# A pipeline of six steps instead of four for the expert tiles of a mixture-of-experts block

## The chip, the core and the metric

The kernel runs on one core of one Trainium2 chip. The metric is the time of one execution on the device in microseconds (us); the median of the runs is what counts. The engines are called by short names. PE is the matrix engine, and PEld its weight load, which overlaps it. DVE is the vector engine, ACT the scalar engine, POOL the GpSimd engine. SP issues DMAs only; SPq and ACTq are the DMA-issuing sides of SP and ACT.

## The reference

The reference is a cross-attention layer and a mixture-of-experts feed-forward layer, each added to its input. The change touches only the second, which is, cut to what matters:

```
def _L0_ffn_ref(x, Wg, W1, W2, W3, Ws1, Ws2, Ws3):
    # T = 4096 tokens, D = 256, H = 128, E = 32 experts, TOP_K = 4
    xf = x.reshape(T, D)
    weights, indices = jax.lax.top_k(softmax(xf @ Wg), TOP_K)
    y = jnp.zeros_like(xf)
    for e in range(E):
        pos = jnp.nonzero(pair_expert == e, size=C, fill_value=P)[0]
        tok, w = ...                      # the tokens that chose e, their weights
        xg = xf[tok]
        out = (silu(xg @ W1[e]) * (xg @ W3[e])) @ W2[e] * w[:, None]
        y = y.at[tok].add(out)
    z = (silu(xf @ Ws1) * (xf @ Ws3)) @ Ws2      # shared expert, 256 wide
    return (y + z).reshape(B, S, D)
```

All numbers are 32-bit floats.

## The kernel before, in words

The 4096 tokens are eight blocks (blk 0 to 7) of 512. Attention runs over all blocks first and lasts to about 390 us of the profile. While it runs, POOL scatters each token's normalised row into a DRAM tensor `xr`, four times, once behind each expert that the token chose. The rows of one expert then lie together and are cut into tiles of 128 rows. There are 128 tiles that are always computed (NM_ = 128), and up to 32 more, in groups of eight, whose number is known only at run time. The inputs at hand need two such groups, 144 tiles in all.

The change lies in the stage that computes those tiles. Each tile passes four functions, named in the list `steps`:

- `expert_in`: PE transposes the 128 by 256 tile of rows `g` into a PSUM bank `pgT` (two instructions); DVE copies it to `gT`.
- `expert_mid`: PE multiplies `gT` by the expert's W1 and W3, side by side, into the bank `peh` (four instructions in the trace); ACT takes Silu of the first half into `h`, DVE multiplies `h` by the second half.
- `expert_turn`: PE transposes `h` into the bank `phT`; ACT copies it to `ehT`.
- `expert_out`: PE multiplies `ehT` by W2 into the bank `py` (two instructions); ACT scales the result by the pair's weight into `y`; POOL scatters `y` with an indirect DMA into the DRAM tensor `ys`, at the place of token and choice.

The loop over `j` is a software pipeline. In iteration j, tile j is in step 0, tile j-1 in step 1, tile j-2 in step 2 and tile j-3 in step 3; a step's result waits in `made` for the next iteration. The program order is kept for every engine: all that is emitted inside `as_written()` runs on its engine in the order in which it was emitted. So each engine is a queue, and a late instruction holds all that stands behind it.

There are two such loops. The first runs over tiles 0 to 127. The second stands inside `tc.Switch`, a branch on the number of further groups, and runs over tiles 128 to 143 here. Between them the pipeline runs empty and is filled again. Other work is placed in the loops by iteration number:

- `fetch(j)` (every eight iterations) makes SP issue eight DMAs, one per tile, that bring the rows of a group of eight tiles into the buffer `g` (two buffers). It also loads the expert numbers into PE's registers.
- `find(j, step)` works out on DVE, in three iterations, the weights `own` and places `place` of a group.
- `shared_in`, `shared_mid`, `shared_out`, `shared_add` compute the shared expert for one block: products `ph` on PE, Silu on ACT, product with the second half on DVE, products `pz` on PE, addition to `y0` on DVE. Their input `sx` is brought back from DRAM by `fetch_shared(blk, engine)`, into one of three buffers of the pool `sxp`. Blocks 1 and 2 are computed in and around the two loops, 3, 4 and 5 in the tail.
- `take(i)` brings the four results of 128 tokens back from `ys` into a buffer `gx` (SP, 512 KB, three buffers). It must wait until the scatters of the tiles concerned have landed: tiles below NE_ = 80 for the first twelve, all tiles below 128 for the next eight. `add_taken` adds a `gx` to `y0` on DVE in three additions, the last of which also issues the next `take`.

After the branch comes the tail. SP gathers the results of the last tokens (`gather`, six DMAs of 1 MB into `gy`), PE computes the shared expert of blocks 3, 4 and 5, DVE adds up, and ACT issues the stores to `out`.

Of the kernel before, what the change touches and what calls it, by code (L numbers as in the profile page):

```python
# [9 lines left out]
F32 = mybir.dt.float32  # L10
# [6 lines left out]
P = 128  # L17
# [13 lines left out]
def kernel(  # L31
# [23 lines left out]
    nc = tc.nc  # L55
# [5 lines left out]
    KC = D // P  # L61
# [4 lines left out]
    H = W1.shape[2]  # L66
# [5 lines left out]
    NM_ = T * TOPK // P  # L72
# [4 lines left out]
    NE_ = NA + NE  # L77
# [3 lines left out]
    RG = 8  # L81
# [15 lines left out]
    def bank(name):  # L97
        return ps.tile([P, 512], F32, tag="bank", name=name)
# [476 lines left out]
    def fetch_shared(blk, engine):  # L575
        sxs[blk] = sxp.tile([P, KC, TB], F32, tag="sx", name=f"sx_{blk}")
        engine.dma_start(sxs[blk], xnd[blk])
# [3 lines left out]
    def shared_in(blk, f, act):  # L581

        if f == 0:
            hTs[blk] = hs.tile([P, HS // P, TB], F32, tag="hT", name=f"hT_{blk}")
        xnT = sxs[blk]
        ph = [bank(f"ph{i}_{blk}_{f}") for i in range(2)]
        for i in range(2):
            for k in range(KC):
                mm = nc.tensor.matmul(  # L589
                    ph[i],  # L590
                    ws13[:, k, i, f * P : (f + 1) * P],
                    xnT[:, k, :],
                    start=(k == 0),
                    stop=(k == KC - 1),
                )
                if i == k == 0:
                    began[0] = mm.ins.name
        sg = hs.tile([P, TB], F32, tag="sg", name=f"sg_{blk}_{f}", bufs=2)

        nc.scalar.activation(sg, ph[0], act, scale=0.5 if act == AF.Tanh else 1.0)  # L600
        sgs[blk, f] = sg, ph, act

    def shared_mid(blk, f):
        sg, ph, act = sgs.pop((blk, f))
        if act == AF.Silu:
            nc.vector.tensor_tensor(hTs[blk][:, f, :], ph[1], sg, ALU.mult)
        else:
            nc.vector.scalar_tensor_tensor(sg, sg, 1.0, ph[0], ALU.add, ALU.mult)
            nc.vector.scalar_tensor_tensor(hTs[blk][:, f, :], sg, 0.5, ph[1], ALU.mult, ALU.mult)
# [468 lines left out]
        sends(3)  # L1078
        shared_add(z)
    late_stack.close()  # L1080
    sxp = ctx.enter_context(tc.tile_pool(name="sxp", bufs=3, side="right"))

    def registers(table, j0, engine, most):
        _, vals = nc.values_load_multi_w_load_instructions(
# [10 lines left out]
    bp = bp_stack.enter_context(tc.tile_pool(name="bp", bufs=2, reuse_waits="tile"))  # L1095
# [60 lines left out]
    def expert_in(j, _):  # L1156
        g = groups[j // RG][0]
        pt = bank(f"pgT_{j}")
        for k in range(KC):
            nc.tensor.transpose(pt[:, k * P : (k + 1) * P], g[:, j % RG, k * P : (k + 1) * P], ident)  # L1160
        gT = bp.tile([P, KC, P], F32, tag="gT", name=f"gT_{j}")
        nc.vector.tensor_copy(gT.rearrange("p k t -> p (k t)"), pt[:, :D])  # L1162
        return gT

    def expert_mid(j, gT):
        ph = bank(f"peh_{j}")
        for k in range(KC):
            nc.tensor.matmul(  # L1168
                ph[:, : 2 * H],
                gT[:, k, :],  # L1170
                we[:, ds(ev[j] * EW + k * 2 * H, 2 * H)],
                start=(k == 0),
                stop=(k == KC - 1),
            )
        h = bp.tile([P, H], F32, tag="h", name=f"h_{j}")
        nc.scalar.activation(h, ph[:, :H], AF.Silu)  # L1176
        nc.vector.tensor_tensor(h, ph[:, H : 2 * H], h, ALU.mult)  # L1177
        return h

    def expert_turn(j, h):  # L1180
        pt = bank(f"phT_{j}")
# [60 lines left out]
    def store(hb, engine=nc.scalar):  # L1242
# [3 lines left out]
            out[r0 : r0 + HC * P, :].rearrange("(c p) d -> p c d", p=P), y0[blk][:, c0 : c0 + HC, :]  # L1246
        )

    steps = [expert_in, expert_mid, expert_turn, expert_out]
    made = {}  # L1250
    BL = BM - 1
    adds, adds_l = (
# [2 lines left out]
    with as_written():  # L1255
        fetch(0)
        fetch_shared(1, nc.sync)
        for j in range(NM_ + len(steps)):
            if j % RG == 1 and j + RG - 1 <= NM_:
                fetch(j + RG - 1)  # L1260
            if j in (4 * RG + 4, 5 * RG + 4, 6 * RG + 4):
                fetch_shared(j // RG - 2, nc.sync)
            if j == NE_ + 3:
                for i in range(3):
                    take(i)
            for i, step in enumerate(steps):
                jj = j - i
                if 0 <= jj < NM_:
                    made[jj, i + 1] = step(jj, made.pop((jj, i), None))
            if j in (2, 5, 8, 11):  # L1270
                next(tz)

            for blk, j0 in ((1, 3), (2, NM_)):
                if j == j0:
                    shared_in(blk, 0, AF.Silu)
                    sends(3)
                if j == j0 + 1:
                    shared_mid(blk, 0)
                    shared_in(blk, 1, AF.Silu)
                    sends(3)  # L1280
                if j == j0 + 2:
                    shared_mid(blk, 1)
            if j == 6:
                shared_out(1)
                sends(2)
            assert not left or j < 6
            if j == 7:
                shared_add(1)
            if NE_ + 8 <= j < NM_:
                for i, step in adds[:1]:  # L1290
                    add_taken(i, step, BE * NC)

                    if step == TOPK // 2 and i % HC == 0 and HC <= i <= 2 * NC:
                        store(i // HC - 1, nc.sync)
                del adds[:1]
            if j < NM_ and j % RG in (0, 1, 2):
                find(j // RG * RG, j % RG)
            if j == NM_ - 2 * RG:
                more = {
                    e: nc.values_load(  # L1300
                        tabs["more"],
                        engines=[e],
                        min_val=0,
                        max_val=(NJ - NM_) // RG,
                        skip_runtime_bounds_check_because="at most as many tiles as are laid out",
                    )
                    for e in mybir.ALL_ENGINES
                }
                tc.switch_hint(more, (NJ - NM_) // RG + 1, label="more")
            if j == NM_ + 2:  # L1310
                fetch_shared(5, nc.scalar)
    assert not adds
    ahead = groups[NM_ // RG][0]
    for n in tc.Switch(more, (NJ - NM_) // RG + 1, hint="more"):
        end = NM_ + n * RG
        groups.clear(), made.clear()
        adds = list(adds_l)
        groups[NM_ // RG] = [ahead]
        del ev[NM_ + RG :]
        with as_written():  # L1320
            for i in range(3):
                take(BE * NC + i)
            for j in range(NM_, end + len(steps)):
                if j % RG == 1 and j + RG - 1 < end:
                    fetch(j + RG - 1)
                for i, step in enumerate(steps):
                    jj = j - i
                    if NM_ <= jj < end:
                        made[jj, i + 1] = step(jj, made.pop((jj, i), None))
                if j < end and j % RG in (0, 1, 2):  # L1330
                    find(j // RG * RG, j % RG)
                if j == end:
                    shared_out(2)
                if j == end + 1:
                    shared_add(2)
                if j >= NM_ + 6:
                    for i, step in adds[: 1 + j % 2]:
                        add_taken(i, step, BL * NC)
                    del adds[: 1 + j % 2]
            for i, step in adds:  # L1340
                add_taken(i, step, BL * NC)
# [26 lines left out]
    with as_written():  # L1368
        come = {hb: gather(hb) for hb in (12, 13, 14, 15, 10, 11)}
        shared_in(3, 0, AF.Silu)  # L1370
        shared_in(3, 1, AF.Silu)
        shared_mid(3, 0)
        store(4)
        shared_mid(3, 1)
        shared_in(4, 0, AF.Silu)
        store(5)
        shared_out(3)
        gathered(*come[12])
        store(12)
        shared_mid(4, 0)  # L1380
        shared_in(4, 1, AF.Silu)
        shared_add(3, store)
        gathered(*come[13])
        store(13)
        shared_mid(4, 1)
        shared_in(5, 0, AF.Silu)
        shared_out(4)
        gathered(*come[14])
        store(14)
        shared_mid(5, 0)  # L1390
        shared_in(5, 1, AF.Silu)
        shared_add(4, store)
        gathered(*come[15])
        shared_mid(5, 1)
        store(15)
        gathered(*come[10])
        shared_out(5)
        gathered(*come[11])
        shared_add(5, store)
# [55 lines left out]
```

## Time and profile before

| what | value |
|---|---|
| median of 3 runs | 764.09 us (763.78 to 767.37) |
| profiled execution, its own time | 762.74 us |
| span of its profile | 761.0 us, so 1.74 us lie around it |
| mean granted clock of PE | 0.989 |
| PE busy | 720.0 us (95%) |
| DVE, ACT, POOL busy | 478.2, 402.3, 404.1 us |
| first and last product of `expert_mid` | 453.9 and 714.8 us |
| last instruction of the two loops on DVE | ends at 723.86 us |
| tail on PE | 724.0 to 754.2 us |

The rows of the profile give a start in us from the span's start, a duration, the engine, the line of the kernel, the operation with its output and input, and in square brackets the idle time of the engine before it with what ended it. "x4" behind a row means that four instructions were merged into it. Matmuls overlap in the pipeline of PE, so a row's duration is longer than the time until the next one starts; the times between starts are what counts.

### The profile page before, as it was taken

Reading aid. Unit: us, or ns where it says so; the run is one execution under the profiler, and the core shown is the slowest. Engines: PE = TensorE matmul, PEld = TensorE weight load, DVE = VectorE, ACT = ScalarE, POOL = GpSimd, SP = SyncE. Lnnn points to the kernel's source line nnn. Section 1 sums busy time; section 2 is a strip of 40 time slices with the busy share of each in tenths; the row PEclk is TensorE's granted clock in tenths of the full one; section 3 lists DMA queues with packets and bytes.
Section 4 is the critical chain, followed back from the end, with each engine's and each line's share of the span. In section 5 each row is a group of like instructions: output and inputs, shape, how many; then the busy total and the mean of one; then the engine's idle time right before and its main releaser. Section 6 shows DMA issues by size and latency. Waiting matters only on the chain. (4 is left out here: it accounts for less than half of the span.)

```text
span 761.0 us, 13078 instructions
## 1 busy us (share of the span) xinstructions
PE 720.0 (95%) x3515; PEld 536.6 (71%) x3515; DVE 478.2 (63%) x1368; ACT 402.3 (53%) x1730; POOL 404.1 (53%) x492
## 2 busy tenths in 40 slices
PE   7999999999999999999987779999999999999996
PEld 5866777677777767777763457788888887876754
DVE  2965565777877878776757433644545466645766
ACT  2658567666777576766553002455555555544310
POOL 1003343346777878777786655565565555553500
PEclk9999999999999999999998989999999999999999
DMA  8930000402217131513136451555746579847594
GB/s 284 342 113 1 1 1 1 132 7 87 100 59 253 47 127 52 170 59 120 74 97 210 140 189 65 159 173 183 224 161 195 166 262 311 258 127 244 186 342 163
DMA packets 78599, 111.98 MB, mean 147 GB/s; under 512 B 8949, under 2 KB 63667, under 8 KB 78515
## 3 DMA queue, kind: packets, MB, share of 16 engines
q1 hardware_dynamic: 60319, 68.76, 29.4%
q0 software_dynamic: 13056, 36.72, 13.0%
q10 hardware_dynamic: 5140, 5.55, 2.1%
q8 instruction: 32, 0.52, 0.3%
q14 instruction: 52, 0.43, 0.2%
HBM read 62.36 MB, written 48.64 MB: 146 GB/s over the span
## 5 line engine op out<-in xcount | busy, mean ns | idle before, releaser
L327 ACT ACTIVATE p<-sc,mx 128x77 f32<-128x77 f32 x512 | 159.5, 352 | 93.2 <-DVE mx L319 93.2
L1197 POOL DMA_INDIRECT ys<-y,place x144 | 138.9, 964 | 124.1 <-ACT y L1196 102.0
L1168 PE MATMUL peh<-we,gT 128*128 x576 | 150.7, 385 | 6.9 <-DVE gT L1162 5.4
L378 PE MATMUL po<-we,pT 128*128 128x256 f32 (+1 forms) x640 | 147.3, 383 | 4.8 <-DVE pT L365 3.4
L555 POOL DMA_INDIRECT xr<-xn,row x128 | 128.1, 1000 | 41.1 <-issue 33.1
L342 POOL TENSOR_TENSOR p<-p,su 128x385 f32<-128x385 f32 (+1 forms) x96 | 91.1, 974 | 97.5 <-DVE su L337 76.5
L311 PE MATMUL sc<-we,qT 128*128 128x385 f32 (+1 forms) x384 | 138.9, 509 | 0.9 <-POOL qT L297 0.9
L378 PEld LDWEIGHTS po<-we,pT 128*128 128x128 f32 (+1 forms) x640 | 118.4, 190 | 27.1 <-DVE pT L365 5.8
L327 ACT ACTIVATION_READ_ACCUMULATOR p<-sc,mx 128x1 f32 x512 | 119.3, 233 | 0.0
L1168 PEld LDWEIGHTS peh<-we,gT 128*128 128x128 f32 x576 | 99.2, 192 | 16.7 <-DVE gT L1162 6.5
L311 PEld LDWEIGHTS sc<-we,qT 128*128 128x128 f32 x384 | 71.1, 189 | 54.3 <-issue 27.7
L1176 ACT ACTIVATE h<-peh 128x128 f32<-128x128 f32 x144 | 40.0, 278 | 116.0 <-PE peh L1168 76.3
L1177 DVE TENSOR_TENSOR h<-peh,h 128x128 f32<-128x128 f32 x144 | 41.9, 291 | 87.1 <-ACT h L1176 80.2
L1192 PE MATMUL py<-we,ehT 128*128 x288 | 86.1, 381 | 0.0
L1196 ACT ACTIVATE y<-py,own 128x256 f32<-128x256 f32 x144 | 68.3, 475 | 17.8 <-PE py L1192 2.0
L319 DVE TENSOR_REDUCE mx<-sc 128x5 f32<-128x385 f32 (+1 forms) x96 | 54.3, 576 | 32.8 <-PE sc L311 30.1
L1162 DVE COPY gT<-pgT 128x256 f32<-128x256 f32 x144 | 60.5, 420 | 19.5 <-PE pgT L1160 9.1
L1160 PE MATMUL pgT<-ident,g 128*128 128x128 f32 x288 | 55.1, 274 | 1.3 <-DMA g<-xr 0.5
L1160 PEld LDWEIGHTS pgT<-ident,g 128*128 128x128 f32 x288 | 40.1, 142 | 17.2 <-issue 2.3
L1192 PEld LDWEIGHTS py<-we,ehT 128*128 128x128 f32 x288 | 43.6, 191 | 11.6 <-issue 0.8
L589 PE MATMUL ph<-sx,ws 128*128 128x512 f32 x96 | 46.0, 628 | 1.6 <-DVE y L1236 1.0
L360 PEld LDWEIGHTS pp<-ident,p 128*128 128x128 f32 x320 | 36.1, 139 | 11.4 <-issue 5.5
(227 smaller groups left out, 927.3 us busy)
## 6 DMA issues: line engine op xcount, KB each, us to landing
g<-xr SPq DMA_DIRECT2D x144, 136.0 KB
gx<-ys SPq DMA_DIRECT2D x20, 512.0 KB
gy<-ys SPq DMA_DIRECT2D x6, 1024.0 KB
xr<-y SPq DMA_DIRECT2D x1, 4352.0 KB
y<-in_x SPq DMA_DIRECT2D x8, 512.0 KB
xnd<-xnT SPq DMA_DIRECT2D x6, 512.0 KB
we<-in_W SPq DMA_DIRECT2D x8, 384.0 KB
out<-y ACTq DMA_DIRECT2D x12, 256.0 KB
```

Source lines behind the costliest of these rows:

```text
L311: nc.tensor.matmul(sc[:, : (h1 - h0) * SK], qTs[blk][:, k, o : o + P], mq[:, b, k, h0 * SK : h1 * SK], start=(k == 0), stop=(k == KC - 1),)
L319: nc.vector.tensor_reduce(mx[:, h0:h1], sv, AX.X, ALU.max, negate=True)
L327: nc.scalar.activation(probs[t][:, h, :], sv[:, h - h0, :], AF.Exp, bias=mx[:, h : h + 1], accum_out=su[:, h : h + 1],)
L342: nc.gpsimd.tensor_tensor(p[:, h0:h1, :], p[:, h0:h1, :], su[:, h0:h1].unsqueeze(2).to_broadcast([P, h1 - h0, SK]), ALU.mult,)
L378: nc.tensor.matmul(po[:, :D], pT[:n, i, :], vo[b][:n, i, :], start=(i == 0), stop=(i == KT - 1))
L555: sct = nc.gpsimd.indirect_dma_start(out=xr, out_offset=bass.IndirectOffsetOnAxis(ap=row[:, i : i + 1], axis=0), in_=xn[:, c, :], in_offse ...
L1160: nc.tensor.transpose(pt[:, k * P : (k + 1) * P], g[:, j % RG, k * P : (k + 1) * P], ident)
L1162: nc.vector.tensor_copy(gT.rearrange("p k t -> p (k t)"), pt[:, :D])
L1168: nc.tensor.matmul(ph[:, : 2 * H], gT[:, k, :], we[:, ds(ev[j] * EW + k * 2 * H, 2 * H)], start=(k == 0), stop=(k == KC - 1),)
L1192: nc.tensor.matmul(py[:, :D], hT, we[:, ds(ev[j] * EW + KC * 2 * H, D)], start=True, stop=True)
L1196: nc.scalar.activation(y, py[:, :D], AF.Identity, scale=own[:, i, 1:2])
L1197: sent = nc.gpsimd.indirect_dma_start(out=ys, out_offset=bass.IndirectOffsetOnAxis(ap=place_[:, i : i + 1], axis=0), in_=y, in_offset=None,)
```

## The change

`steps` gets two more entries. A new function, `expert_rest`, hands its input on and issues nothing; it stands once behind `expert_in` and once behind `expert_mid`. In iteration j, tile j is transposed, tile j-2 gets its first products, tile j-4 is turned and tile j-5 leaves. `gT` and `h` get three buffers each instead of two; the pool `sxp` has two buffers instead of three. The loops run two iterations longer at their ends, and what hung on iteration numbers is moved:

- `fetch_shared(4)` is no longer issued from SP in iteration 52, but from ACT in iteration 130, where `fetch_shared(5)` was; that one is issued from ACT in the tail, behind the two `shared_in` of block 3, whose buffer it takes.
- the first `take` moves from iteration 83 to 85, and the additions of taken results from 88..127 to 90..129.
- `shared_out(2)` and `shared_add(2)` move from the first and second iteration behind the last tile to the fifth and sixth.

```
-    sxp = ctx.enter_context(tc.tile_pool(name="sxp", bufs=3, side="right"))
+    sxp = ctx.enter_context(tc.tile_pool(name="sxp", bufs=2, side="right"))
...
-        gT = bp.tile([P, KC, P], F32, tag="gT", name=f"gT_{j}")
+        gT = bp.tile([P, KC, P], F32, tag="gT", name=f"gT_{j}", bufs=3)
...
-        h = bp.tile([P, H], F32, tag="h", name=f"h_{j}")
+        h = bp.tile([P, H], F32, tag="h", name=f"h_{j}", bufs=3)
...
+    def expert_rest(j, it):
+
+        return it
...
-    steps = [expert_in, expert_mid, expert_turn, expert_out]
+    steps = [expert_in, expert_rest, expert_mid, expert_rest, expert_turn, expert_out]
...
-            if j in (4 * RG + 4, 5 * RG + 4, 6 * RG + 4):
+            if j in (4 * RG + 4, 5 * RG + 4):
                 fetch_shared(j // RG - 2, nc.sync)
-            if j == NE_ + 3:
+            if j == NE_ + 5:
                 for i in range(3):
                     take(i)
...
-            if NE_ + 8 <= j < NM_:
+            if NE_ + 10 <= j < NM_ + 2:
                 for i, step in adds[:1]:
                     add_taken(i, step, BE * NC)
...
             if j == NM_ + 2:
-                fetch_shared(5, nc.scalar)
+                fetch_shared(4, nc.scalar)
...
-                if j == end:
+                if j == end + 4:
                     shared_out(2)
-                if j == end + 1:
+                if j == end + 5:
                     shared_add(2)
...
         shared_in(3, 0, AF.Silu)
         shared_in(3, 1, AF.Silu)
+        fetch_shared(5, nc.scalar)
         shared_mid(3, 0)
```

## Prediction

> **What bounds the kernel now.** I read the engines' busy time by stretches first. In the middle of the expert stage the first two numbers say all: PE is busy 136.00 of 136.00 us, at the full clock.
>
> ```profile
> 487.00:623.00 136.00, 136.00 (x754) 114.94 (x753) 69.19 (x234) 76.16 (x252) 78.88 (x82) 1.00 0.61 194
> ```
>
> The timeline of PE there repeats every 1.63 us: 0.22 (pgT) + 0.87 (peh) + 0.11 (phT) + 0.43 (py) between starts. The six-step order issues the same instructions in the same order, only of older tiles, so these 136 us don't move. What can move is where the period is longer, or PE waits. The timeline of PE, and of DVE and ACT where they hold it:
>
> ```profile
> 453.85 1.97 PE L1168 MATMUL peh<-we,gT 128*128 x4 [3.90 <-DVE gT L1162]
> 481.35 1.13 PE L1168 MATMUL peh<-we,gT 128*128 x4 [1.10 <-DVE eq L1122]
> 628.89 0.28 ACT L1176 ACTIVATE h<-peh 128x128 f32<-128x128 f32 x1 [2.44 <-PE peh L1168]
> 629.55 0.33 PE L1182 MATMUL phT<-ident,h 128*128 128x128 f32 x1 [1.04 <-DVE h L1177]
> 688.41 1.13 PE L1168 MATMUL peh<-we,gT 128*128 x4 [0.69 <-DVE gT L1162]
> 699.79 0.41 PE L1160 MATMUL pgT<-ident,g 128*128 128x128 f32 x2 [0.55 <-DMA g<-xr]
> ```
>
> In four of these PE waits for gT or h, which the change makes a step earlier; in the last one for rows from DRAM. Then the chain that ended last: it doesn't begin on PE, but on SP's queue, and it passes through the fetch of tiles 136 to 143. The line before the final PE row is DVE's last addition inside the branch; PE's second product of block 3 starts 0.14 us behind it.
>
> ```profile
> 699.04 3.56 DMA g<-xr
> 702.60 0.33 DVEq L1122
> ...
> 703.84 0.34 DVE gT L1162
> 704.19 0.04 issue
> 704.23 1.13 PE peh L1168 x4
> ...
> 723.43 0.43 DVE y L1236
> 723.86 0.14 issue
> 724.00 8.82 PE ph L589 x20
> ```
>
> Why that fetch is late: SP's queue holds the takes of iteration 128 before it, and these wait for the last scatter of tile 127 (POOL 688.07). SP resumes at 692.13, issues three gx, then g from 694.41; tile 136 is transposed at 699.79, 11.72 us after that scatter began.
>
> **Part by part, first loop.** The rests issue nothing. In the steady state gT is ready 1.0 us before its product (copy ends 501.15, product 502.16) and h 0.83 us before its transpose (500.57 to 501.40); both get 1.63 us more.
> Start: the third tile's two transposes move into the wait that ends at 453.85 (the late `shared_add` on DVE ahead of gT isn't touched). They cost 0.42 at 455.61. Bounds 0.2 to 0.4, I take 0.3.
> At 481.35 the period is 2.97 instead of 1.63; DVE's eight table operations had delayed gT by less than the new slack: 1.34 gone.
> At 628.89 ACT is 2 us late and the period is 3.41: 1.78. Here only part goes: the copy to ehT stands behind the same late Silu and has no step of rest, and its product would wait from 628.46 to about 629.35. 0.9 stays, 0.88 goes (nothing to 1.78, should the late Silu fall elsewhere).
> Seven periods of 1.70 to 1.73 (478.38, 483.08, 632.62, 644.62, 646.35, 655.20, 656.93) are DVE backlog: 0.64 in all.
> The periods of 2.15 at 639.66 and 2.24 at 653.48 follow PE's register loads in iterations 105 and 113, ahead of its transposes: they stay. Sum of the first loop: 0.3 + 1.34 + 0.88 + 0.64 = 3.16.
>
> What else moves there costs nothing, with these covers. The first takes stand two iterations later on SP's queue, ahead of the fetch for tile 96: its issue goes from 608.14 to about 608.5 (605.11 + 3.26 - 1.6 for the gx, 1.3 to issue them, 0.4 to 0.9 until the fetch). Tile 96 is due at 620.4, and 11.72 us would still be met. sx 4 leaves SP (0.46 us at 547.07) and takes the slot of sx 5 on ACT's queue. Its buffer is that of block 2, whose products end before it is issued; it is needed 40 us later. One buffer less in `sxp` makes block 3 wait for block 1, read by about 470 and refilled at 534. The additions have 40 iterations as before. POOL's scatters come two iterations later and POOL is idle 0.67 us in each.
>
> **The emptying before the branch.** `shared_in(2)` now stands ahead of the last turns, so nothing covers them: turn, out, turn, out, out are 2x0.11 + 3x0.43 = 1.51 us of PE. ACT must copy ehT, scale y (0.47), copy and scale again in that order; counted with the rows at 499.77 to 500.52, the last product ends 2.08 after the first turn: 0.57 lost. So tile 127 leaves PE at 687.12 - 3.16 + 0.57 = 684.5 instead of 687.12. POOL gets three results at once (0.96 + 0.30 each, as at 624.44 and 625.74). Its last scatter starts 1.94 us behind PE, at 686.5; before it was 0.95.
>
> **The branch.** Up to the transposes of tile 136 PE now has 8 transposed tiles, 6 first products, 4 turns, 3 outs: 1.74 + 5.20 + 0.43 + 1.30 = 8.67 us, and about 0.64 until the first gT is copied as at 688.41: it is through at 693.8. The rows come 11.72 us after the scatter, at 698.2. PE stands 4.4 us, where it stood 0.55. Behind that it has 8 transposed tiles, 10 first products, 12 turns, 13 outs and `shared_out(2)`: 1.74 + 8.67 + 1.28 + 5.63 + 3.45 = 20.77, with 0.57 for the uncovered turns 21.34. It ends at 719.5. The wait of 0.78 at 704.23 (DVE held by `find` until all rows had landed) is gone, for gT is two iterations ahead.
> The end: DVE has `shared_add(2)` and two additions left, 1.8 us after PE, where six additions ran from 719.87 to 723.86 before. Block 3's second product starts at 719.5 + 1.95 = 721.5 instead of 724.00: 2.5 us gained. The tail keeps its 37.0 us.
>
> **sx 5 in the tail.** ACT issues it when block 3 is read, 5.2 us into the tail; it is needed 10.3 us later, at 739.55 on the old clock. Alone, at 687.40, 0.45 of its 0.52 MB were through by 690: about 3.3 us. Beside the gathers, ACT's queue moved 0.26 MB from 731 to 735 in 1 KB packets while SP's moved 1.24 in 4 KB ones. At that worst share it takes 8 us plus the landing, about 10: just in time. With 4 KB packets I take 5 to 6 us: cost nothing. ACT's wait before the issue delays only a store and no Silu, since the next is due 1.8 us later.
>
> Sum: 761.0 - 2.5 = 758.5 of span, 760.2 with the 1.74 around it. This execution lay 1.35 below the median, so the forecast is 764.09 - 2.5 = **761.6**. Own range 759.5 to 763.8: the gain of the first loop can be 1.2 to 4.2, the landing 1 us either way.
>
> **The clock.** The 4.4 us that PE stands could cost more than themselves. Granted clock by half microseconds:
>
> ```profile
> 453.50:454.00 0.50, 0.15 (x1) 0.15 (x2) 0.50 (x3) 0.00 (x0) 0.00 (x0) 1.00 0.00 0
> 454.00:454.50 0.50, 0.50 (x2) 0.41 (x3) 0.23 (x1) 0.00 (x0) 0.00 (x0) 0.51 0.00 0
> ```
>
> After idle times of 4.57 (to 437.03) and 3.90 (to 453.85) the clock was 0.50 for 3.3 us, a loss of 1.65. The falls are at 436.95, 454.0 and 757.9, and their distances are 5 and 89 times 3.41: the clock is judged at fixed beats, and a beat has to be idle nearly whole (3.25 of 3.41 at 454.0). An idle time of 4.4 holds such a beat in about a third of the cases, so I leave the loss out of the sum.
> The Trainium skill ("TensorE: Matmul & The Clock Gate", its table of practical rules) speaks against the change more bluntly: no idle gaps of PE above some 3 us between bursts, since one idle window halves the clock. By that rule the sum would be 763.3; by the beats of the trace it is 761.6. The phase of the next run decides, and no row can give it.
>
> **The rivals.**
> The clock falls at tile 136: 761.6 + 1.65 = 763.3. For it: both long waits before tiles did so. Against: the beat. 0.20.
> The rows of tile 136 are not late: the takes are through sooner, or the scatter lands faster when nothing else moves. PE keeps its 4.4 us: 757.2. For it: the landing to SP at the branch's end took only 1.6 us (722.84 to 724.43), against 3.1 here. Against: three gx, 1.5 MB, stand before g either way. 0.12.
> Slower than before: sx 5 comes late. If it waits behind all gathers (6.28 MB, through at about 744.2 by the bytes per stretch) it lands at 745.7, 6.1 behind 739.55, and the clock falls too: 761.6 + 6.1 + 1.65 = 769.4. It decides from 10.3 us after issue. Against: the stores on ACT's queue moved while gathers did. 0.12.
> The stalls return elsewhere: late instructions with no cause in the profile (2.19 at 452.78 on DVE, 2 us at 628.89 on ACT) fall at other places, and the slack of ehT, which got no rest, is used up: gain eaten, 764 to 766. 0.10.
> The forecast holds with 0.46.
>
> **Chances.** A measurement tells about 0.5% here, 3.8 us: 760.3 and 767.9 are the marks. Faster: the rows in time, 0.12, and the lower quarter of the forecast, 0.12: 0.24. Slower: sx 5, 0.12, and a fifth of the returned stalls, 0.02: 0.14. Within: 0.62. The range from 757.0 to 767.5 leaves out half of the rows in time (0.06) and sx 5 (0.12).
>
> **What would show it.** Right: no wait at the fellows of 481.35; tile 136's transposes with an idle time of 3 to 5 us on a DMA; tile 127's scatter about 2 us behind its product; `shared_out(2)` last before the tail; DVE's last addition within 2 us of it; no wait in block 5's first product. Wrong: PE waits for ehT in many periods, a period other than 1.63 in the middle, or the tail longer than 37 us.

## The result, and the profile after

The changed kernel is slower by 0.39%: 766.53 us median of 20 runs (762.21 to 771.62) against 762.84 of 20 runs of the kernel before (760.51 to 767.37), ratio 1.0039, 95% interval 1.002 to 1.0057. The forecast was 761.6, which was 2.5 us below the median of three runs at hand then (764.09); the time lies 3.7 us above the kernel before. The profiled execution took 764.69 us, its span is 762.9, its mean granted clock 0.984 (762.74, 761.0 and 0.989 before).

The busy time by stretches first: the middle of the stage is what it was, PE busy without a gap at the full clock (the number in third place from the end).

```profile
487.00:623.00 136.00, 136.00 (x754) 114.89 (x753) 68.53 (x235) 75.80 (x251) 79.72 (x83) 1.00 0.59 190
```

Then PE's timeline, the rows with the waits.

```profile
446.52 1.22 PE L617 MATMUL pz<-ws,hT 128*128 128x256 f32 x2 [4.29 <-DVE hT L606]
...
456.27 1.13 PE L1168 MATMUL peh<-we,gT 128*128 x4 [2.35 <-issue]
...
630.00 0.70 PE L1196 MATMUL py<-we,ehT 128*128 x2 [0.81 <-ACT ehT L1188]
...
699.78 0.41 PE L1160 MATMUL pgT<-ident,g 128*128 128x128 f32 x2 [2.93 <-DMA g<-xr]
...
724.24 1.10 PE L589 MATMUL ph<-sx,ws 128*128 128x512 f32 x2 [1.21 <-DVE y L1240]
```

The wait at 481 is gone, the late Silu at 629 now costs 0.81 us (before ehT), and tile 136 waits for its rows, all as the prediction had it. But PE waits 4.29 us at 446.52, where the same products began without a wait before (at 445.21; the wait of 4.57 ahead of them, at 437.03, is 2.34 here). The first product stands at 456.27 and not at 453.85, although DVE, which it waits for, has nothing new to do ahead of it, and PE only the third tile's two transposes. The wait at 446.52 isn't DVE's alone: ACT, DVE and POOL all pause and begin again within 0.03 us of each other, with no releaser that the profile can name.

```profile
445.77 0.69 DVE L606 TENSOR_TENSOR hT<-ph,sg 128x512 f32<-128x512 f32 x1 [10.82 <-issue]
445.80 0.60 ACT L600 ACTIVATE sg<-ph 128x512 f32<-128x512 f32 x1 [6.01 <-remote]
445.79 0.96 POOL L555 DMA_INDIRECT xr<-xn,row  x1 [2.93 <-remote]
```

And in front of block 3 PE waits for DVE with both products. Two rows more show the end of the first loop, the last product of tile 127 on PE and the start of its scatter on POOL:

```profile
686.18 0.70 PE L1196 MATMUL py<-we,ehT 128*128 x2 [0.27 <-ACT ehT L1188]
688.61 0.96 POOL L1201 DMA_INDIRECT ys<-y,place  x1 [0.30 <-issue]
```

The granted clock by half microseconds shows what the wait at tile 136 cost beside itself. PE is idle from 696.85 to 699.78, and the clock is halved for the beat from 700.9 to 704.3:

```profile
700.50:701.00 0.50, 0.50 (x4) 0.40 (x3) 0.15 (x1) 0.00 (x0) 0.00 (x0) 0.90 1.09 398
...
703.50:704.00 0.50, 0.50 (x2) 0.30 (x2) 0.50 (x3) 0.00 (x0) 0.41 (x1) 0.50 0.12 49
704.00:704.50 0.50, 0.50 (x3) 0.41 (x2) 0.50 (x2) 0.17 (x1) 0.00 (x0) 0.69 0.13 49
704.50:705.00 0.50, 0.50 (x5) 0.40 (x5) 0.50 (x3) 0.39 (x3) 0.00 (x0) 1.00 0.65 230
```

The chain that ended last shows the same place: PE's work carries it to 694, then the fetch, then slow products (the four of peh take 1.71 us of the chain, where 0.87 is usual).

```profile
693.82 0.54 PE peh L1168 x3
694.36 5.29 DMA g<-xr
699.65 0.14 issue
699.78 0.41 PE pgT L1160 x2
...
702.59 1.71 PE peh L1168 x4
```

**Time lost at half clock.** Each run has its time and its mean granted clock. From them I work out, for a set of runs, the time lost, (1 - clock) x time, and the net time, time - lost. A beat of 3.41 us at half clock loses 1.7. (This counts lost time as if all of it lay on the path. Ahead of the expert tiles, where PE waits anyway, it costs less, and behind PE's last product nothing: there the profiles of before and after lose 1.6 and 2.0 us.) The runs went to chips of two kinds: on the slower ones the kernel before takes 762 to 765 us, on the faster ones 746 to 747 (medians). Both kernels, on one chip of each kind (means):

| chip | kernel | us | clock | lost | net |
|---|---|---|---|---|---|
| slower | before (27 runs) | 764.57 | 0.9870 | 9.94 | 754.63 |
| slower | after (12) | 768.87 | 0.9815 | 14.22 | 754.65 |
| faster | before (23) | 746.62 | 0.9948 | 3.86 | 742.76 |
| faster | after (12) | 745.84 | 0.9923 | 5.72 | 740.12 |

On the faster chip the net time falls by 2.64 us, close to the forecast's 2.5, and 1.86 come back as time lost. On the slower chip the net time doesn't fall and 4.28 us more are lost. So there are two things to find: the clock, and what differs on the slower chips.

### The profile page after: what moved, and what is told of

Read it like the earlier page. It is cut to its first block, busy times and chain, and to the rows that moved or that the text cites. A ratio compares the mean times of both kernels' runs of the same rounds, so it can differ in the third digit from the quotient of the medians.

```text
span 762.9 us, 13052 instructions
## 1 busy us (share of the span) xinstructions
PE 721.8 (95%) x3515; PEld 538.6 (71%) x3515; DVE 477.3 (63%) x1368; ACT 401.8 (53%) x1730; POOL 405.0 (53%) x492
## 4 chain that ended last, share of the span: by engine, by line
PE 78%; DVE 7%; ACT 6%; issue 4%; POOL 2%; DMA 1%; DVEq 0%; another core or an unknown queue 0%; ACTq 0%; POOLq 0%
PE peh L1168 16%; PE po L378 15%; PE sc L311 13%; PE py L1196 8%; PE ph L589 6%; ACT p L327 5%; PE pgT L1160 4%; PE pz L617 3%; PE pp L360 2%; PE phT L1186 2%; PE pvT L684 1%; POOL xr L555 1%; DVE mx L319 1%; PE pm L708 1%; PE pvo L708 1%
```

## The experiments

Three theories stood at the start. A: the loss arises at the branch, by the wait at tile 136 and the half clock behind it. B: it arises ahead of the first product. C: it is the moved `fetch_shared` of blocks 4 and 5.

**e1 to e4, on a slower chip: the branch, its entry, and the sx moves.**

`e1_six_fetch_first`, the changed kernel with the fetch of tiles 136 to 143 ahead of the takes:

```
         with as_written():
-            for i in range(3):
-                take(BE * NC + i)
             for j in range(NM_, end + len(steps)):
                 if j % RG == 1 and j + RG - 1 < end:
                     fetch(j + RG - 1)
+                if j == NM_ + 1:
+                    for i in range(3):
+                        take(BE * NC + i)
```

> Six steps, but inside the branch SP issues the fetch of tiles 136 to 143 ahead of the three takes instead of behind them. Theory A (the loss is made at the branch: PE stands ahead of tile 136, 2.9 us in the profile after, and then runs 3.4 us at half clock): the wait goes, the clock stays full there, the run is 3 to 5 us shorter than the changed kernel, about 762, level with the kernel before or a little under it, and the mean clock is higher. Theory B (the loss lies ahead of the first expert product, which came 2.4 us later in the profile after although the code there is the same): less than 3 us, since only the wait itself can go, and the first product is late here too. Theory C (the loss is made in the tail, by sx 5 or the wait of both first products for DVE): under 1 us.

Ratio to the kernel before 1.0007 (0.9973 to 1.0042). The wait at tile 136 is gone; a wait of 2.36 us at the branch's entry takes its place in the profile (put down there to the landing of sx, which the transposes that wait don't read). The loss against the kernel before is no longer clear of noise: 0.9 us in the means of the runs, so some 2.8 of the 3.7 are gone, on the edge between A and B. The clock (mean 0.9845) is still 0.0034 below that kernel's, 2.6 us more lost at half clock, though in its profile the clock stays full from 462 us to the end of PE's work.

`e2_four_fetch_first`, the same move in the four-step kernel before:

> Four steps, with the same fetch ahead of the takes. Theory A: the waits of 0.55 us ahead of tile 136 and 0.78 us at the next product go, 1 to 1.5 us gained on the kernel before; the gain is smaller than with six steps because the shorter pipeline has more work of PE between the branch and tile 136. Theories B and C say nothing on this one beyond 0 to 1.5 us.

0.9962 (0.9941 to 0.9982): faster than before, by the order of two groups of DMAs alone. The waits of 0.55 and 0.78 us at tile 136 are gone.

`e3_six_covered`, the changed kernel with block 2's shared products two iterations later, so that they cover the last turns:

```
-            for blk, j0 in ((1, 3), (2, NM_)):
+            for blk, j0 in ((1, 3), (2, NM_ + 2)):
...
-            if j == NM_ + 2:
+            if j == NM_ + 4:
                 fetch_shared(4, nc.scalar)
```

> Six steps, with the two shared_in of block 2 two iterations later, so that they lie between the last turns of the first loop and cover them (fetch_shared 4 moves behind them). Theory A: 0.6 us of PE, and the last scatter of tile 127 starts 0.95 instead of 2.0 us behind PE, so that the rows of tile 136 come 1.6 us earlier: 1 to 2 us shorter than the changed kernel, and fewer half-clock beats behind tile 136. Theories B and C: 0.6 us at most.

1.004 (1.0012 to 1.0067), as slow as the changed kernel. The emptying is covered, tile 136 now waits longer, and two beats at half clock follow (698.1 to 704.9).

```profile
698.95 0.66 PE L1160 MATMUL pgT<-ident,g 128*128 128x128 f32 x2 [3.44 <-DMA g<-xr]
```

So the 0.57 us of the uncovered emptying were only part of a sum that ends at the rows of tile 136.

`e4_four_sx_tail`, the kernel before with only the change's two moves of sx and two buffers in `sxp`:

> Four steps, of the change only the moves of the shared expert's inputs: sxp with two buffers, sx 4 issued from ACT in iteration 130, sx 5 in the tail. Theories A and B: level with the kernel before within 1 us, no wait in block 5's first product. Theory C: 2 to 4 us slower, with a wait of PE for sx 5 near 740 us.

0.998 (0.9956 to 1.0004). Theory C falls: these moves cost nothing.

**e5 to e8, on a faster chip: which loop, and idle products.** `e5_six_then_four` keeps six steps in the first loop only, `e6_four_then_six` in the branch only. The edit of e5 (e6 is the reverse, with takes and additions as before):

```
+        steps = [expert_in, expert_mid, expert_turn, expert_out]
         with as_written():
...
-                if j == end + 4:
+                if j == end:
                     shared_out(2)
-                if j == end + 5:
+                if j == end + 1:
                     shared_add(2)
```

> Six steps in the first loop, four in the loop of the branch (shared_out(2) and shared_add(2) back to the first and second iteration behind the last tile); the rest is the changed kernel. Mean over runs so far: the kernel before 762.7 us at a clock of 0.9877, the changed kernel 766.3 at 0.9822. Theory A (the loss is at the branch: the six-step loop reaches tile 136 too early, PE waits there and a half-clock beat follows): four steps put 2.6 us more of PE work ahead of tile 136 (1 first product, 1 turn, 1 out more, 1.41 us, and no uncovered end), so the wait at tile 136 is at most 1.5 us, the clock is 0.986 to 0.988 and the time 761 to 763. Theory B (the loss arises ahead of or in the first loop): the clock stays at 0.982 to 0.983 and the time at 765 to 767.

The times and clocks expected for e5 and e6 were those of a slower chip; what counts here is the distance from the kernel before.

1.0015 (0.9993 to 1.0036), clock 0.9910. No wait at tile 136; instead PE is done with the branch early and waits 2.64 us for DVE's additions in front of block 3, with a beat at half clock behind it.

> The reverse: four steps in the first loop, with the takes and additions where the kernel before has them, six steps in the loop of the branch. Theory A: the emptying is covered again, but tile 136 has only the six-step loop's work ahead of it, so its transposes wait 2 to 4 us for rows, the clock is 0.983 to 0.986 and the time 764 to 768, for the first loop's gains are missing too. Theory B: the clock is that of the kernel before, 0.987 to 0.988, and the time 761 to 763.

0.9994 (0.9983 to 1.0006), clock 0.9928. The longest wait of all at tile 136 and a beat behind it, and yet level with the kernel before: what the wait takes, the quicker end of the branch gives back (block 3 starts right behind `shared_out(2)`).

```profile
684.63 0.66 PE L1160 MATMUL pgT<-ident,g 128*128 128x128 f32 x2 [4.61 <-DMA g<-xr]
```

`e7_six_warm`, ten products without use ahead of tile 136, and `e8_four_ff_warm`, ten in three places ahead of the expert tiles:

```
+    def warm(n, name):
+        pt = bank(f"warm_{name}")
+        for _ in range(n):
+            nc.tensor.matmul(pt[:, : 2 * P], ident, ws13[:, 0, 0, :], start=True, stop=True)
...
+                if j == NM_ + RG:
+                    warm(10, f"{n}_{j}")
```

> The changed kernel, and ahead of the two transposes of tile 136 ten products 128x256 of resident data into a spare bank that nobody reads: 10 x 0.217 = 2.2 us of PE work where the profiled run waited 2.93 us. They change no result. If the idle time as such costs (theory A with the clock): the wait left is about 0.8 us, no half-clock beat at 700 to 704, clock 0.984 to 0.985, 764 to 765. If only the lateness of the rows costs, or the loss is at the start (theory B): clock 0.982 and 766 to 767.

> The four-step kernel whose fetch of tiles 136 to 143 stands ahead of the takes (760.06 us at a clock of 0.9877), with ten such idle products in each of three waits ahead of the expert tiles: in front of shared_out(0), of shared_out(z) and of the first peh. The profile of the kernel before waits 4.57 and 3.90 us there and runs at half clock for 3.3 us behind each. If these beats lie on the path: clock 0.990 to 0.992, 757 to 759. If PE is held by DVE there anyway, or the beats come from other idle times: 760 to 761, clock 0.988 to 0.990. If the dummies stand in the way of work: up to 6.5 us slower, 762 to 766.

e7: 1.0055 (1.0032 to 1.0079); e8: 1.0115 (1.0099 to 1.0131). Both were mis-sized. A product of this width is two instructions, so ten took 4.4 us and not 2.2:

```profile
678.70 4.48 PE L584 MATMUL warm<-ws,ident 128*128 128x256 f32 x20
```

In e7 PE came through 4.31 us after it began them, later than the rows. In its profile there is no wait and no half clock at tile 136 (746.67 us, mean clock 0.997), but eight of its eleven runs show 0.986 to 0.991 and take 751 to 755 us, which this doesn't explain. In e8 there was nothing to fill: on the faster chip PE doesn't wait there (e6 has no wait above 1.5 us between 425 and 680 us), and the 13 us of idle products stood in the way. Neither tells the theories apart.

**e9 to e12, on a second slower chip.** `e9_six_again` is the changed kernel, `e10_six_warm2` has the idle products also behind `shared_out(2)`, `e11_four_then_six_ff` is e6 with the fetch ahead of the takes, `e12_five_in` has the first rest alone:

```
-    steps = [expert_in, expert_rest, expert_mid, expert_rest, expert_turn, expert_out]
+    steps = [expert_in, expert_rest, expert_mid, expert_turn, expert_out]
```

> The changed kernel itself, beside the three that follow and the kernel before, on the same chip. The runs so far came from two chips: on the first the kernel before takes 762.5 us, on the second 747.0, with the first expert product at 453.85 and 440.32 us; the changed kernel has run on the first alone. Theory D, formed from six_then_four and six_warm (both with more time at half clock than the kernel before, 6.7 and 6.6 us lost against 4.1, whether or not tile 136 is covered): six steps bring PE further ahead of the chain scatter, take, addition, so it waits either at tile 136 or for DVE's last addition in front of block 3, and each wait can cost beats at half clock. It expects a clock 0.003 to 0.005 below that of the kernel before and a time 2 to 4 us above, on any chip. Theory B' (the loss is the first chip's late instructions ahead of the first product): on the second chip equal to before within 1 us.

1.0056 (1.0027 to 1.0084); theory D's numbers. But the profile has a second place. PE waits 9.78 us for the first gT, and the clock is halved for three beats, from 452.5 to 462.7 (for the first 6.2 us of them PE stands anyway). On DVE nothing explains it: these are its rows, two of them late without a releaser that the profile can name ("remote"), and PE's product behind them.

```profile
447.61 0.69 DVE L632 TENSOR_TENSOR y<-pz,y 128x512 f32<-128x512 f32 x1 [2.71 <-PE pz L617]
455.40 0.69 DVE L632 TENSOR_TENSOR y<-pz,y 128x512 f32<-128x512 f32 x1 [7.10 <-remote]
458.20 0.42 DVE L1162 COPY gT<-pgT 128x256 f32<-128x256 f32 x1 [2.10 <-remote]
...
458.68 2.08 PE L1168 MATMUL peh<-we,gT 128*128 x4 [9.78 <-DVE gT L1162]
```

> The changed kernel with ten idle products ahead of tile 136 (as in six_warm) and ten more behind shared_out(2), the last work of the branch on PE, in front of the wait for DVE's last addition (1.21 us in the changed kernel's profile, 1.66 in six_warm's, 2.64 in six_then_four's). Theory D: the clock comes back to that of the kernel before (within 0.001), and the time to within 1 us of it or up to 1 us below; the dummies stand 1 us beyond the wait at the most. If the lost beats arise in the first loop or ahead of it: the clock stays 0.003 or more below, and the time is that of six_warm (751.7 us on the second chip) plus 0.5 to 1.

1.0141 (1.0096 to 1.0186), wrong for both: 8.8 us of idle products, and a wait of 4.37 us at the branch's entry (694.97, <-issue) that no other profile from that chip has. It says nothing on theory D.

> Four steps in the first loop, six in the loop of the branch, and the fetch of tiles 136 to 143 ahead of the takes. four_then_six waited 4.61 us at tile 136 and ran 3.4 us at half clock behind it, and was still level with the kernel before. With the rows in time both should go: clock that of the kernel before (within 0.001), time 2 to 4 us below the kernel before, by theory D; if the wait only moves to DVE's last addition, no more than 1 us below.

0.9946 (0.992 to 0.9971), clock 0.9870, that of the kernel before. As theory D expected (a lead over the chain of data turns into waits, unless that chain is moved too): with the rows in time the kernel gains 4 us. How much of it is the order of the DMAs alone, as in e2, and how much the six steps of the branch, wasn't tried on one chip. No wait above 0.5 us is left from the branch's entry to block 3:

```profile
689.24 1.13 PE L1168 MATMUL peh<-we,gT 128*128 x4 [0.47 <-DVE gT L1162]
715.30 3.62 PE L617 MATMUL pz<-ws,hT 128*128 128x256 f32 x16
718.75 5.50 PE L589 MATMUL ph<-sx,ws 128*128 128x512 f32 x12
```

> One rest alone, behind the transposes: five steps in both loops, shared_out(2) and shared_add(2) in the fourth and fifth iteration behind the last tile, first take in iteration 84, additions in iterations 89 to 128; the rest is the changed kernel. The waits for gT go, those for h stay. Theory D: PE is ahead by nearly as much as with six steps (1.34 of the 1.78 us that the changed kernel's loop gained lay at gT), so the loss is at least half that of the changed kernel: 1 to 3 us above the kernel before, clock 0.002 to 0.004 below. If the second rest (behind the first products) is what costs: level with the kernel before or below.

1.003 (1.0007 to 1.0053), clock 0.9815. One rest is enough to lose: tile 136 waits 3.41 us and pays two beats, and the first product stands at 457.99.

**e13 to e15, back on the first slower chip: the start of the loop.** Theory E: on the slower chips the rests also lose where the pipeline is filled. PE has the transposes of three tiles and one product, and then nothing until DVE, which is late there, has made the second gT. In the profiles on slower chips up to here, time lost between 430 and 465 us was 3.4 to 5.1 us with four steps at the start (kernel before, e2, e4, e11) and 5.1 to 6.8 with five or six (after, e1, e3, e9, e10, e12).

```
+    def at(jj):
+        return (0, 2, 4, 5) if jj >= 16 else (0, 1, 2, 3)
...
-            for i, step in enumerate(steps):
-                jj = j - i
-                if 0 <= jj < NM_:
-                    made[jj, i + 1] = step(jj, made.pop((jj, i), None))
+            for i, step in enumerate(four):
+                for jj in range(max(j - 5, 0), min(j + 1, NM_)):
+                    if j - jj == at(jj)[i]:
+                        made[jj, i + 1] = step(jj, made.pop((jj, i), None))
```

`e13_six_from_16` is this; `e14_six_to_16` has `jj < 16` and the branch of the kernel before; `e15_six_middle_ff` has `16 <= jj < NM_ - 8` and the fetch ahead of the takes.

> The changed kernel, but the first 16 tiles of the first loop go through in four steps (offsets 0, 1, 2, 3) and only those behind them in six (0, 2, 4, 5); branch, takes and additions as in the changed kernel. Theory E: the first rests lose at the start of the loop. In six profiles with six or five steps in the first loop on the two slower chips the first product starts at 455.33 to 458.68 us with one exception (452.50, and its second product then at 456.11); in four with four steps at 453.54 to 455.06. By E the first product comes back to 453.5 to 455, the loss falls by 2 to 3 us, and what is left is the wait at tile 136: level with the kernel before to 1.5 us above it. If the start only varies by chance and the branch alone is at fault (theory A): 3 to 4 us above, as the changed kernel.

0.9995 (0.9967 to 1.0023), clock 0.9864 beside 0.9866 of the kernel before: the loss is gone, though tile 136 still waits. The changed kernel's own 1.0039 and 1.0056 were measured at other times (the kernel before moved from 762.32 to 764.45 us on this chip between e1 and e13), and the first of the two intervals meets this one at 1.002, so this speaks for E without settling it.

```profile
452.08 1.13 PE L1168 MATMUL peh<-we,gT 128*128 x4 [0.94 <-issue]
...
698.46 0.66 PE L1160 MATMUL pgT<-ident,g 128*128 128x128 f32 x2 [2.95 <-DMA g<-xr]
```

> The mirror image: the first 16 tiles in six steps, all behind them and the branch in four, takes, additions, shared_out(2) and shared_add(2) where the kernel before has them; three buffers for gT and h, two in sxp. Theory E: first product at 455.5 to 458.5 on a slower chip, 2 to 4 us above the kernel before. Theory A: level with it (within 1 us), first product at 453.5 to 455.

1.0045 (1.0014 to 1.0077), theory E's number, but not clean. The start lost 6.8 us at half clock, as E has it, but the first product came at 454.69, earlier than E has it (the second tile's at 458.22). Then the step back to four at tile 16 costs too: the eight iterations there take 17.2 us, 2.2 more than the 13.0 and the 1.95 us of work that the change of step count draws together, and the eight behind them again 1.9 more than 13.0, with a beat at half clock from 511:

```profile
508.68 1.13 PE L1168 MATMUL peh<-we,gT 128*128 x4 [0.74 <-issue]
511.05 0.35 PE L1182 MATMUL phT<-ident,h 128*128 128x128 f32 x1 [1.25 <-DVE h L1177]
```

> Four steps for the first 16 and the last 8 tiles of the first loop, six for those between and in the branch, and the fetch of tiles 136 to 143 ahead of the takes. It takes away both suspected losses and keeps the gains of the first loop behind tile 16 (1.34 at 481, 0.9 at 629, 0.6 of backlog in the profile of before). four_then_six_ff, without these gains, was at 0.9946 of the kernel before. Theories A and E together expect 2 to 3 us less than that: 0.991 to 0.993. If being ahead only turns into a wait for DVE at the end of the branch: 0.994 to 0.997.

0.9984 (0.9957 to 1.0011): a miss by 0.5%. It goes back to four steps at tile 120, and there the profile has a loss like that of e14: from iteration 120 to the branch's first it takes 27.2 us, where e11 takes 21.4 and 1.95 of work are drawn together, 3.8 more. A beat at half clock lies here too:

```profile
684.02 0.47 PE L1186 MATMUL phT<-ident,h 128*128 128x128 f32 x1 [1.93 <-DVE h L1177]
```

The profiles of e13 and e15, which start with four steps, lost 3.4 us each at half clock between 430 and 465 us.

**e16 to e18, on a second faster chip.** `e16_six_third` is the changed kernel, `e17_six_from_4` is e13 with `jj >= 4`, `e18_six_from_16_ff` is e13 with the fetch ahead of the takes.

> The changed kernel again, beside the next two on the same chip: they differ from it in single points and the chips differ in the start. 3 to 4.5 us above the kernel before on a slower chip (1.0039 and 1.0056 so far).

0.9986 (0.9972 to 1.0). The expectation was for a slower chip; on this kind of chip the changed kernel isn't slower. The first product waits 0.46 us only, so there is no late DVE; tile 136 waits as ever, and a beat at half clock follows (682 to 685.5).

```profile
440.88 1.13 PE L1168 MATMUL peh<-we,gT 128*128 x4 [0.46 <-DVE gT L1162]
...
681.77 0.42 PE L1160 MATMUL pgT<-ident,g 128*128 128x128 f32 x2 [2.88 <-DMA g<-xr]
```

> The changed kernel, but its first four tiles go through in four steps; from the fifth tile on, and in the branch, six. It differs from the changed kernel in the order of the first iterations alone. Theory E in its sharp form (the loss lies where the pipeline is filled: transposes of three tiles, one product and then nothing that could run while DVE is late with the second copy to gT; seven profiles with rests there lose 5.0 to 6.8 us at half clock between 430 and 465 us, six without 3.4 to 5.1): 2 to 4 us below the changed kernel, within 1.5 us of the kernel before, clock 0.002 to 0.004 above the changed kernel's. If the loss is spread over the first 16 tiles or lies elsewhere: as the changed kernel within 1 us.

1.0012 (1.0002 to 1.0021), slower than e16 and not faster. The chip had no late start to cure, so E wasn't tried by it. Its own loss is a late start of PE at the branch's entry, with half clock behind:

```profile
673.42 1.76 PE L1160 MATMUL pgT<-ident,g 128*128 128x128 f32 x6 [4.27 <-issue]
```

Three profiles have a wait above 2 us there: e1, e10 and e17. In these three, and in none of the 17 others, two loads of 8 KB of instructions start in the last 2.4 us before PE begins tile 128. So PE may have waited for its code; no run tried it.

> six_from_16 with the fetch of tiles 136 to 143 ahead of the takes, so without the wait at tile 136 (2.95 us there and 1.7 lost at half clock), and without the step back to four at tile 120 that cost six_middle_ff a wait of 1.93 us and a beat at half clock. Both causes are then gone by the changed kernel's own means: 2 to 4 us below the kernel before, 0.995 to 0.997; the wait at the branch's entry for sx (2.36 us in six_fetch_first) eats 1 to 2 us of 4.6. If being ahead is of no use: level with the kernel before.

0.9949 (0.9934 to 0.9963), 743.2 us: faster than the kernel before and than the changed kernel beside it (745.81). Time lost is 3.42 us (before 3.86), the net time 3.1 below. No wait over 0.5 us is left from the branch's entry to block 3, where DVE's last addition still holds PE:

```profile
671.71 0.63 PE L1160 MATMUL pgT<-ident,g 128*128 128x128 f32 x4 [0.41 <-issue]
702.95 3.24 PE L589 MATMUL ph<-sx,ws 128*128 128x512 f32 x7 [1.21 <-DVE y L1240]
```

e18 and e11 are the two best versions; they ran on chips of different kinds and weren't compared with each other, nor with e2, the kernel before with the same order of DMAs. So what the six steps add to that order isn't shown.

## Why the prediction was wrong

**The step that failed: the clock that was left out of the sum.** The prediction saw that PE would stand at tile 136, but left the 1.65 us for the clock out of the sum, because a beat had to be idle nearly whole (3.25 of 3.41 us). That condition was wrong. PE stood for 2.93 us, of which 2.3 fell into the beat from 697.5 to 700.9, 67% of it, and the next beat ran at half clock. Set against PE's idle times in all 20 profiles, behind 425 us, the beats show a limit near half: the clock fell behind each of the 33 beats that were idle for more than 57%, and behind none that was idle for less than 51%. The profile before couldn't show where the limit lies: between 30 and 749 us its beats are idle for 40% at most or for 90% and more (the latter three times; the fall at 413.05 us is one that the prediction doesn't list). A wait of 4.4 us covers at least 2.2 us of some beat, 64%. So by these figures the fall was certain, where the prediction gave it a third.

Counted by waits: behind tile 120 the 20 profiles have ten waits of PE of 2.6 us or more (after 2.93, e3 3.44, e5 2.64, e6 4.61, e9 2.91, e10 4.37, e12 3.41, e13 2.95, e16 2.88, e17 4.27), and half clock follows each of the ten, in e3 and e12 for two beats. Of six from 1.6 to 2.4 us (e1 2.36, e7 1.66, e8 1.83, e9 2.27, e13 2.29, e15 1.93) one was followed by it (e15). The term should have stood in the sum with nearly its full 1.65. On the faster chip, where the net time fell by 2.64 us, 1.86 more were lost. The rule that was quoted from the Trainium skill ("TensorE: Matmul & The Clock Gate", its table of practical rules, no gaps above some 3 us) was the better guide, and the runs are stricter still: 2.64 us were enough, and once 1.93.

**How far each part was off, in the profiled run.** Block 3's second product was forecast at 721.5 and began at 726.03, 4.5 us late. The first loop brought 0.5 us and not 2.6: tile 127 left PE at 686.6, against 687.1 before and 684.5 forecast. With that the rows of tile 136 came at 699.78 and not at 698.2: 1.6. From there to the end of `shared_out(2)` took 23.25 us and not 21.34: 1.9, of which 1.7 is the beat at half clock. The end of the branch took 3.0 us and not 1.95: 1.0. These are two single executions; over the runs the difference is larger, +3.7 us instead of -2.5.

**The start: 0.3 gained became a loss, on the slower chips.** Iteration 24 begins (DVE's `eq`) at a mean of 507.86 us in four slower-chip profiles with four steps (kernel before, e2, e4, e11) and of 506.35 in five with six (after, e1, e3, e9, e10), which have 1.95 us less work done by then: 508.30. So the start with the stall at 481 gained nothing, where 0.3 + 1.34 were forecast; it is 0.4 behind. Counted from the first product, the two gains are there on the faster chip: iteration 24 begins 51.75 us behind it with four steps (e6) and 48.01 + 1.95 = 49.96 with six (e16), 1.8 gained. What fails is the arrival of the first product, after late instructions of DVE, and the half clock beside it. On slower chips the first product comes at a mean of 454.1 us with four steps at the start (six profiles, 452.1 to 455.1) and of 456.0 with five or six (seven, 452.5 to 458.7): these ranges overlap. The time lost at half clock between 430 and 465 us parts the two better: 3.4 us in five of the six and 5.1 in e2, against 5.1 to 6.8 in all seven. e13 speaks for it that with four steps there the loss goes; e14 mixes it with another loss, and e17 met a chip without it. Why DVE is late on these chips, and whether the rests make it later or only make its lateness cost more, stays open: its work ahead is the same, the profile names no releaser, and in the profile after other engines pause with it.

**The end of the branch was mis-sized by 1.0 us.** I let block 3's first product run before DVE's last addition and only the second wait, 1.95 us behind `shared_out(2)`. In the changed kernel both wait: 1.21 us for DVE and then the first product's own time, 3.0 in all. From the second product on the tail keeps its 37 us (36.9), as forecast. With four steps in the first loop and six in the branch (e6, e11) neither product waits; with five in both (e12) the second alone does, for 0.22 us. What in the first loop decides it wasn't found.

**What was right.** The middle of the stage, 136.00 of 136.00. The wait at 481 gone, and 0.81 left at 629 (0.9 forecast). The emptying took 2.02 us from the last turn but one to the end (2.08), and POOL's last scatter began 2.0 us behind PE (1.94). The rows came 11.17 us behind that scatter (11.72), and PE took 0.9 us more to reach them than worked out (two late starts, 0.29 and 0.63): hence 2.93 and not 4.4. The moves of sx cost nothing (e4). The gain of 2.5 us is what is left on the faster chip when the lost time is taken out. That is partly luck: the end of the branch costs more than forecast there too (the same 1.21 us for DVE in e16), and the wait at tile 136 less (2.88).

**The rivals.** "The clock falls" was the right one, but not to its end: 763.3 is the sum for the start as forecast, and the slower chips add what the start lost. "The stalls return elsewhere" named the late DVE instruction at 452.78 as a cause that could fall elsewhere; that they come in the fill of the pipeline was not in it.

## What to carry to other kernels

A deeper pipeline moves the leading engine ahead of its data; price the next wait for data together with the clock that a long wait costs, and move the transfer that ends it first: here two groups of DMAs in another order gave 0.4% by themselves, and 0.5% in the two best versions with six steps in the branch, on other chips. It may pay to let the pipeline start shallow and to deepen it later: one comparison speaks for it (e13, where DVE is late at the start and deepening at tile 16 cost 0.2 us in the profile). Stepping back to four lost some 4 us in both profiles that did it. A gain of 0.3% that is read from one profile should be tried on more than one chip.

## What the runs showed of the hardware

The same program takes 762 to 765 us on two chips and 746 to 747 on two others (medians). In one profile of each kind 13.5 us of that lie ahead of the first product (453.85 us in the profile before, 440.32 in e6), and they gather where instructions of DVE begin late, most of them without a releaser: 6.0 of them at one instruction (434.67 us in the profile before, 6.23 idle there against 0.19).

A product 128x256 of 32-bit floats is two instructions of 0.217 us.

The clock of PE is set for beats of 3.41 us that lie fixed in time. Behind 425 us a beat with PE idle for 51 to 57% of its time was followed by half clock in four cases of nine, one idle for more always and one idle for less never. At half clock a beat that was itself idle for 19% or more was followed by another (14 of 14), one idle for 17% or less by the full clock (37 of 37). So one wait of 3.4 us can cost two beats when it reaches into the second (e3, 698.1 to 704.9, idle for 25% of the first halved beat; e12, 703.5 to 710.3, for 30%).
